# Fifteen rectified copies for a piecewise-linear GELU, on ScalarE in place of GpSimd

## The chip, the core and the metric

The kernel runs on one core of a Trainium2 chip. A core has engines with queues of their own: PE (TensorE, matrix products), DVE (VectorE), ACT (ScalarE), POOL (GpSimd) and SP (SyncE, which here only issues transfers). Each works through its own instructions in order and waits for the others by semaphores. All data that they work on lie in on-chip memory, 128 partitions wide; the products of PE land in PSUM. The metric is the time of one execution on the device in microseconds (us), and of several executions the median.

## The reference

The program is a chain of twelve residual steps on an x of 128 tokens by 256 features, in four layers of three steps: cross attention against a context of 12544 rows, self attention, and a feed-forward. Everything is in float32. The step that is changed is the feed-forward of the third layer (called l2f, since layers count from 0):

```python
_PWL_X = jnp.linspace(-4.0, 4.0, 33, dtype=jnp.float32)
_PWL_Y = 0.5 * _PWL_X * (1.0 + jax.lax.erf(_PWL_X / jnp.sqrt(jnp.float32(2.0))))
...
y = jnp.interp(xq, _PWL_X, _PWL_Y)
y = jnp.where(xq > 4.0, xq, jnp.where(xq < -4.0, jnp.float32(0.0), y))
...
h = jnp.einsum('bsd,df->bsf', x, w1) + b1
h = float2fix(h, MANT_BITS)
h = pwlin_gelu_basic(h, MANT_BITS, MANT_BITS)
h = float2fix(h, MANT_BITS)
out = jnp.einsum('bsf,fd->bsd', h, w2) + b2
return float2fix(out, MANT_BITS)
```

`float2fix` rounds to multiples of 1/256. The hidden width is 1024, so h has 128 tokens by 1024 values. The GELU is a broken line with a kink every 0.25 from −4 to 4.

## The kernel before

`Net` keeps x in on-chip memory and runs the twelve steps one after the other. Each step begins with a layer norm of x (`norm`, L271: statistics on DVE, a square root on ACT, and at L279 the scaled result on DVE), and turns it over to have features on partitions (`transposed`, L282). Products go through `mm` (L303). At the end `add_to_x` (the addition at L341) makes the new x. So a step can't start its own computation before the step ahead of it has ended.

What can run ahead are the keys and values of the four cross attentions (l0x, l1x, l2x, l3x), which depend on the context alone. They are split into jobs (`project`, L184): PE products, an ACT pass with a bias for the keys (L202), and POOL's transfers to scratch in device memory (L206 for keys, L230 for values). Jobs are taken from a list by `pump` (L136): within the cross attentions at given rates, and in the steps between them one job per PSUM bank asked for (`one`, L121). `weight` (L249) loads the weights of a step through POOL's transfer queue, two entries of the plan ahead, into three buffers; a load waits until the last reader of its buffer is done.

A cross attention (`cross`) first computes the queries, then scores of four groups of heads against 25 blocks of 512 context rows: maxima (score products at L447, reduced by DVE at L460), then the scores again, transposed (L495), exponentials on ACT (L508) and products with the values (L542). Before that POOL clears tiles for the keys (`clear`, memset at L392, 128x1024 each, up to 17 of them), zeroes small ones (L376, L380), and SP loads the keys back (L408).

The feed-forward l2f works on tiles of 128x1024, hidden features on partitions and tokens along the row, eight chunks of 128. It writes the broken line as an even part and a linear part. With a = min(|h|, 4) and kinks at 0, 0.25, ..., 3.75, it starts from y = h/2 and adds c_i · max(a − at_i, 0) for each of the sixteen kinks. The kink at zero needs no rectified copy, since a is never negative. For the other fifteen, POOL makes the copy (L1082) in a tile of the pool `l2f_r`, which has two buffers, and DVE adds it into y (L1084). Each sum needs the sum before it, and each copy needs a buffer that a sum has left. A mask `far` (L1074, L1088) replaces the result by max(h, 0) beyond 4 (L1086, L1087, L1090, L1091). Then y is rounded (`fixed`, L1043 and L1045), and sixteen matrix products give the output l2f_o, after which l3x begins.

The order of instructions on each engine is the program's order, but a scheduler moves instructions of different streams between each other: on POOL eight key transfers of l3x stand between the copies, one behind each pair.

Of the kernel before, what the change touches and what calls it, by code (L numbers as in the profile page):

```python
# [10 lines left out]
F32 = mybir.dt.float32  # L11
I32 = mybir.dt.int32
AF = mybir.ActivationFunctionType
ALU = mybir.AluOpType
# [4 lines left out]
P = 128  # L19
# [49 lines left out]
def _gelu_kinks():  # L69

    at = [0.25 * i for i in range(17)]
    even = [0.5 * a * math.erf(a / math.sqrt(2.0)) for a in at]
    slope = [(even[i + 1] - even[i]) / 0.25 for i in range(16)]
    return [(at[i], slope[i] - (slope[i - 1] if i else 0.0)) for i in range(16)]


class Net:
    def __init__(self, ctx, tc, io):
        self.tc, self.nc, self.io = tc, tc.nc, io
        nc = self.nc  # L80
        cp = ctx.enter_context(tc.tile_pool(name="const", bufs=1))
        self.small = ctx.enter_context(tc.tile_pool(name="small", bufs=2))
        self.xp = ctx.enter_context(tc.tile_pool(name="x", bufs=2))
        self.wp = ctx.enter_context(tc.tile_pool(name="w", bufs=3))
        self.bp = ctx.enter_context(tc.tile_pool(name="bg", bufs=2))
        self.dp = ctx.enter_context(tc.tile_pool(name="scratch", bufs=1, space=DRAM))
        self.ps1 = ctx.enter_context(tc.tile_pool(name="ps1", bufs=1, space=PSUM))
        self.psa = ctx.enter_context(tc.tile_pool(name="psa", bufs=1, space=PSUM))

        self.x = self.xp.tile([P, D], F32, name="x0", tag="x")  # L90
        nc.sync.dma_start(out=self.x, in_=io["x"])
        self.cst = cp.tile([P, NCONST], F32, name="cst", tag="cst")
        nc.sync.dma_start(out=self.cst, in_=io["cst"])
        self.cols = cp.tile([P, NCOL], F32, name="cols", tag="cols")
        nc.scalar.dma_start(out=self.cols, in_=io["cols"])
        self.rows = cp.tile([P, NROW], F32, name="rows", tag="rows")
        nc.gpsimd.dma_start(out=self.rows, in_=io["rows"].to_broadcast([P, NROW]))
        self.eps = {}
        for e in (EPS, 1e-6):
            t = cp.tile([P, 1], F32, name=f"eps{len(self.eps)}", tag=f"eps{len(self.eps)}")  # L100
            nc.vector.memset(t, e)
            self.eps[e] = t
        self.ident = self.const("ident")

        self.plan, self.tiles, self.loaded = [], {}, 0
        self.jobs, self.every, self.count, self.side = [], 0, 0, False
        self.turn, self.done = 0, set()
# [940 lines left out]
    def l2_ffn(self):  # L1048

        nc = self.nc  # L1050
        with self.tc.tile_pool(name="l2f", bufs=1) as pool, \
                self.tc.tile_pool(name="l2f_r", bufs=2) as rp:
            xn, xnT = self.normed(pool, "l2f")
            w1 = self.weight(("w_l2f1", None)).rearrange("p (c f) -> p c f", c=2)
            w2 = self.weight(("w_l2f2", None)).rearrange("p (c f) -> p c f", c=8)
            h = pool.tile([P, 8, P], F32, name="l2f_hs", tag="h")
            for i in range(2):
                ps = self.one(f"l2f_h{i}")
                for f in range(4):
                    ws = slice((4 * i + f) * P, (4 * i + f + 1) * P)  # L1060
                    self.mm(ps[:, f * P : (f + 1) * P], [w1[:, c, ws] for c in range(2)],
                            [xnT[:, c, :] for c in range(2)])
                b1 = self.col("l2f_b1")[:, 4 * i : 4 * i + 4]
                nc.vector.tensor_tensor(
                    out=h[:, 4 * i : 4 * i + 4, :], in0=ps.rearrange("p (c t) -> p c t", c=4),
                    in1=b1.unsqueeze(2).to_broadcast([P, 4, P]), op=ALU.add)
            h = h.rearrange("p c t -> p (c t)")
            self.fixed(h, h)

            a = pool.tile([P, 1024], F32, name="l2f_a", tag="a")  # L1070
            nc.vector.scalar_tensor_tensor(out=a, in0=h, scalar=-1.0, in1=h, op0=ALU.mult,
                                           op1=ALU.max)
            far = pool.tile([P, 1024], F32, name="l2f_far", tag="far")
            nc.vector.tensor_scalar(out=far, in0=a, scalar1=4.0, scalar2=None, op0=ALU.is_gt)  # L1074
            nc.vector.tensor_scalar(out=a, in0=a, scalar1=4.0, scalar2=None, op0=ALU.min)
            y = pool.tile([P, 1024], F32, name="l2f_y", tag="y")
            nc.vector.tensor_scalar(out=y, in0=h, scalar1=0.5, scalar2=None, op0=ALU.mult)
            for i, (at, c) in enumerate(_gelu_kinks()):
                t = a
                if i:  # L1080
                    t = rp.tile([P, 1024], F32, name=f"l2f_k{i}", tag="k")
                    nc.gpsimd.tensor_scalar(out=t, in0=a, scalar1=-at, scalar2=0.0, op0=ALU.add,  # L1082
                                            op1=ALU.max)
                nc.vector.scalar_tensor_tensor(out=y, in0=t, scalar=c, in1=y, op0=ALU.mult,  # L1084
                                               op1=ALU.add)
            nc.vector.tensor_scalar(out=h, in0=h, scalar1=0.0, scalar2=None, op0=ALU.max)  # L1086
            nc.vector.tensor_tensor(out=h, in0=h, in1=far, op=ALU.mult)  # L1087
            nc.vector.tensor_scalar(out=far, in0=far, scalar1=-1.0, scalar2=1.0, op0=ALU.mult,  # L1088
                                    op1=ALU.add)
            nc.vector.tensor_tensor(out=y, in0=y, in1=far, op=ALU.mult)  # L1090
            nc.vector.tensor_tensor(out=y, in0=y, in1=h, op=ALU.add)  # L1091
            self.fixed(y, y)
            ps = self.one("l2f_o")
            self.mm(ps[:, :D], [y[:, f * P : (f + 1) * P] for f in range(8)],
                    [w2[:, f, :] for f in range(8)])
            o = pool.tile([P, D], F32, name="l2f_os", tag="o")
            nc.vector.tensor_tensor(out=o, in0=ps[:, :D], in1=self.row("l2f_b2"), op=ALU.add)
            self.fixed(o, o)
            self.add_to_x([o], "l2f")
# [321 lines left out]
```

## Time and profile before

| | |
|---|---|
| median of 3 timed runs | 2828.08 us (2827.34 to 2830.71) |
| profiled execution, its own time | 2820.92 us |
| its span, first to last instruction | 2819.2 us |
| mean clock granted to TensorE | 0.931 of full |
| busy: PE, DVE, ACT, POOL | 2574.5, 1586.2, 1128.1, 695.3 us |
| between 2165 and 2256 us: PE, DVE, ACT, POOL busy | 14.33, 39.65, 3.52, 69.03 us |
| the same stretch: granted clock, share of the transfer engines | 0.57, 0.15 |

The first rows are for the whole program. The last two are for the stretch that holds l2f, 91 us long. In the profile a line such as L1084 is the line of the kernel before. A group of instructions is written as output<-inputs with shapes; "busy, mean ns" is their own time, and "idle before" is how long their engine stood still ahead of them and what released it. The chain that ended last is followed back from the last instruction of the program, at each step to what released it; "issue" in it is time for which the profile names no releaser.

### The profile page before, as it was taken

To read this page: it belongs to the slowest core of one execution; us is meant where nothing else is said; L and a number is where in the kernel's file an instruction comes from. 1 tells how busy PE (TensorE), PEld (TensorE's weight loads), DVE (VectorE), ACT (ScalarE), POOL (GpSimd) and SP (SyncE) were. 2 spreads that over 40 slices of the span, in tenths; PEclk is the share of its full clock that TensorE was granted. 3 is DMA by queue.
4 is the path that set the end of the run, shared out by engine and by line. 5 is a ranking of instruction groups with operands and counts; after the bars stand their busy time and mean duration, and the time that the engine had idled before them with its cause. 6 is when DMAs were issued, how large, how long until landed. Compare 5 with 4: busy or idle time off the path is not lost. (4 is left out here: it accounts for less than half of the span.)

```text
span 2819.2 us, 76052 instructions
## 1 busy us (share of the span) xinstructions
PE 2574.5 (91%) x32135; PEld 1882.8 (67%) x32135; DVE 1586.2 (56%) x3135; ACT 1128.1 (40%) x2076; POOL 695.3 (25%) x1287
## 2 busy tenths in 40 slices
PE   7999999998999999999998987999997089999978
PEld 4556887876745666666666555788886056888857
DVE  2445666413165788888776329666633376666422
ACT  1112555562202444444761340355564002555653
POOL 5775000014425222212123332000002824000001
PEclk9998999999978999999999995899999569999989
DMA  7875232226756766677544553222323034222216
GB/s 258 244 212 161 72 105 80 64 85 214 231 178 196 227 194 210 195 208 199 166 141 129 175 177 87 87 83 72 85 63 116 23 90 130 73 81 79 59 37 211
DMA packets 186355, 387.47 MB, mean 137 GB/s; under 512 B 32460, under 2 KB 88992, under 8 KB 181920
## 3 DMA queue, kind: packets, MB, share of 16 engines
q1 hardware_dynamic: 134064, 219.94, 25.9%
q0 software_dynamic: 51584, 161.42, 19.2%
q8 instruction: 255, 4.18, 0.6%
q10 hardware_dynamic: 368, 1.25, 0.1%
q14 instruction: 84, 0.69, 0.1%
HBM read 276.31 MB, written 112.58 MB: 138 GB/s over the span
## 5 line engine op out<-in xcount | busy, mean ns | idle before, releaser
L508 ACT ACTIVATE l1x_e<-l1x_e 128x512 f32<-128x512 f32 (+1 forms) x400 | 239.4, 621 | 254.7 <-DVE l1x_e L503 253.7
L460 DVE TENSOR_REDUCE l0x_mxs<-l0x_s 128x1 f32<-128x512 f32 (+1 forms) x400 | 243.7, 672 | 150.9 <-PE l0x_s L447 150.0
L455 DVE CUSTOM_DVE_ANT_0 l1x_j<-l1x_s,l1x_f 128x512 f32<-128x512 f32 (+1 forms) x400 | 271.5, 679 | 72.9 <-PE l1x_s L447 27.1
L460 DVE TENSOR_REDUCE l3x_mxs<-l3x_s 128x1 f32<-128x512 f32 (+1 forms) x400 | 242.4, 671 | 104.7 <-PE l3x_s L447 103.8
L508 ACT ACTIVATE l2x_e<-l2x_t 128x512 f32<-128x512 f32 (+1 forms) x400 | 206.4, 597 | 226.9 <-PE l2x_t L495 225.2
L460 DVE TENSOR_REDUCE l2x_mxs<-l2x_s 128x1 f32<-128x512 f32 (+1 forms) x400 | 241.9, 671 | 95.1 <-PE l2x_s L447 94.2
L503 DVE TENSOR_TENSOR l1x_e<-l1x_t,l1x_g 128x512 f32<-128x512 f32 (+1 forms) x400 | 249.6, 673 | 62.5 <-ACT l1x_e L508 31.2
L508 ACT ACTIVATE l0x_e<-l0x_t 128x512 f32<-128x512 f32 (+1 forms) x400 | 206.3, 597 | 163.6 <-PE l0x_t L495 161.9
L508 ACT ACTIVATE l3x_e<-l3x_t 128x512 f32<-128x512 f32 (+1 forms) x400 | 206.2, 597 | 156.8 <-PE l3x_t L495 155.1
L495 PEld LDWEIGHTS l1x_t<-l1x_qb,l1x_kt 32*128 32x128 f32 x3136 | 171.1, 187 | 81.3 <-ACT l2x_vs L225 27.6
L495 PE MATMUL l0x_t<-l0x_qb,l0x_kt 32*128 32x128 f32 x3136 | 206.1, 283 | 5.8 <-ACT l0x_e L508 5.8
L495 PE MATMUL l2x_t<-l2x_qb,l2x_kt 32*128 32x128 f32 x3136 | 205.9, 283 | 5.7 <-ACT l2x_e L508 5.6
L495 PE MATMUL l3x_t<-l3x_qb,l3x_kt 32*128 32x128 f32 x3136 | 204.7, 283 | 5.8 <-ACT l3x_e L508 5.8
L495 PE MATMUL l1x_t<-l1x_qb,l1x_kt 32*128 32x128 f32 x3136 | 204.7, 285 | 4.2 <-ACT l2x_vs L225 1.2
L495 PEld LDWEIGHTS l0x_t<-l0x_qb,l0x_kt 32*128 32x128 f32 x3136 | 178.0, 187 | 39.6 <-issue 21.8
L495 PEld LDWEIGHTS l2x_t<-l2x_qb,l2x_kt 32*128 32x128 f32 x3136 | 177.9, 187 | 38.9 <-issue 21.4
L495 PEld LDWEIGHTS l3x_t<-l3x_qb,l3x_kt 32*128 32x128 f32 x3136 | 176.8, 186 | 38.4 <-issue 20.4
L447 PE MATMUL l2x_s<-l2x_kt,l2x_qb 32*128 32x512 f32 (+1 forms) x800 | 200.3, 741 | 0.5 <-issue 0.5
L447 PE MATMUL l3x_s<-l3x_kt,l3x_qb 32*128 32x512 f32 (+1 forms) x800 | 194.7, 695 | 2.3 <-ACT l3x_ks L202 1.8
L206 POOL DMA_DIRECT2D l3x_kx<-l3x_ks x208 | 100.1, 489 | 332.0 <-ACT l3x_ks L202 294.1
L447 PE MATMUL l0x_s<-l0x_kt,l0x_qb 32*128 32x512 f32 (+1 forms) x800 | 176.7, 654 | 4.5 <-ACT l0x_ks L202 4.5
L447 PE MATMUL l1x_s<-l1x_kt,l1x_qb 32*128 32x512 f32 (+1 forms) x800 | 173.3, 657 | 3.2 <-DMA l1x_kt<-l1x_kx 1.9
(609 smaller groups left out, 4058.2 us busy)
## 6 DMA issues: line engine op xcount, KB each, us to landing
l1x_f<-in_fside SPq DMA_DIRECT2D x96, 256.0 KB
l1x_g<-in_fsideT SPq DMA_DIRECT2D x96, 256.0 KB
w<-in_w_l3f POOLq DMA_DIRECT2D x16, 1024.0 KB, 5.1
l0x_kt<-l0x_kx SPq DMA_DIRECT2D x192, 72.0 KB
l1x_kt<-l1x_kx SPq DMA_DIRECT2D x192, 72.0 KB
l2x_kt<-l2x_kx SPq DMA_DIRECT2D x192, 72.0 KB
l3x_kt<-l3x_kx SPq DMA_DIRECT2D x192, 72.0 KB
l0x_vx<-l0x_vs POOLq DMA_DIRECT2D x24, 544.0 KB, 7.2
```

The costliest lines, as they stand in the source:

```text
L206: nc.gpsimd.dma_start(out=kx[8 * half + h, 2:18, :], in_=t["k"][16 * h : 16 * h + 16, :n])
L447: nc.tensor.matmul(banks[j][:, :m], qb[g][r, :], t[r, at : at + m], start=True, stop=True)
L455: nc.vector.tensor_tensor_reduce(out=junk[:, :m], in0=banks[j][:, :m], in1=ft[k][:, :m], scale=1.0, scalar=-3.0e38, op0=ALU.add, op1=ALU.m ...
L460: nc.vector.tensor_reduce(out=mxs[g][:, j, i : i + 1], in_=banks[j][:, :m], axis=AX.X, op=ALU.max)
L495: nc.tensor.matmul(banks[j][:, a * P : (a + 1) * P], t[r, at + a * P : at + (a + 1) * P], qb[g][r, :], start=True, stop=True)
L503: nc.vector.tensor_tensor(out=e[:, j, :m], in0=src, in1=gt[k][:, : m // P, :].rearrange("p a q -> p (a q)"), op=ALU.add)
L508: nc.scalar.activation(e[:, j, :m], src, AF.Exp)
```

## The change

There are three edits. A constant tile `kinks` of 128x16 is filled at the start by POOL, one column per kink with the value −at_i, which stands on POOL's queue ahead of the first weight loads. The pool of the rectified copies gets three buffers in place of two, 4 KB per partition more. The copies are made by ACT as Relu(a + bias), with a column of `kinks` as the bias, where POOL computed max(a − at_i, 0). The sums on DVE and everything on PE stay as they are, in the same order; on ACT the fifteen copies come between the last key pass ahead of l2f_o and the square root of l3x's norm.

```diff
         self.ident = self.const("ident")
+        self.kinks = cp.tile([P, 16], F32, name="kinks", tag="kinks")
+        for i, (at, _) in enumerate(_gelu_kinks()):
+            nc.gpsimd.memset(self.kinks[:, i : i + 1], -at)
...
         with self.tc.tile_pool(name="l2f", bufs=1) as pool, \
-                self.tc.tile_pool(name="l2f_r", bufs=2) as rp:
+                self.tc.tile_pool(name="l2f_r", bufs=3) as rp:
...
                 t = a
                 if i:
                     t = rp.tile([P, 1024], F32, name=f"l2f_k{i}", tag="k")
-                    nc.gpsimd.tensor_scalar(out=t, in0=a, scalar1=-at, scalar2=0.0, op0=ALU.add,
-                                            op1=ALU.max)
+                    nc.scalar.activation(t, a, AF.Relu, bias=self.kinks[:, i : i + 1])
                 nc.vector.scalar_tensor_tensor(out=y, in0=t, scalar=c, in1=y, op0=ALU.mult,
                                                op1=ALU.add)
```

## The prediction

> **What bounds the kernel now.** I read the page first, from the top: busy times, then the 40 slices of 70.5 us.
>
> ```profile
> PE 2574.5 (91%) x32135; PEld 1882.8 (67%) x32135; DVE 1586.2 (56%) x3135; ACT 1128.1 (40%) x2076; POOL 695.3 (25%) x1287
> ...
> PE   7999999998999999999998987999997089999978
> ...
> ACT  1112555562202444444761340355564002555653
> POOL 5775000014425222212123332000002824000001
> PEclk9998999999978999999999995899999569999989
> ```
>
> Over the whole span PE decides. One slice contradicts this: the 32nd (2185 to 2255 us) has PE at 0, ACT at 0 and POOL at 8. It is the second layer's feed-forward (l2f), where the change is made. So I left the averages and asked for the groups of instructions between 2175 and 2256 us (busy and mean | idle before, and who ended it), and for VectorE's timeline there.
>
> ```profile
> L1082 POOL TENSOR_SCALAR l2f_k<-l2f_a 128x1024 f32<-128x1024 f32 x15 | 60.2, 4023 | 8.2 <-DVE l2f_a L1075 7.8
> L1084 DVE SCALAR_TENSOR_TENSOR l2f_y<-l2f_k,l2f_y 128x1024 f32<-128x1024 f32 x15 | 23.4, 1557 | 38.3 <-POOL l2f_k L1082 38.3
> ```
>
> ```profile
> 2180.39 2.05 DVE L1084 SCALAR_TENSOR_TENSOR l2f_y<-l2f_a,l2f_y 128x1024 f32<-128x1024 f32 x1
> 2182.37 0.68 DVE L1088 TENSOR_SCALAR l2f_far<-l2f_far 128x1024 f32<-128x1024 f32 x1
> 2183.99 2.05 DVE L1084 SCALAR_TENSOR_TENSOR l2f_y<-l2f_k,l2f_y 128x1024 f32<-128x1024 f32 x1 [0.94 <-POOL l2f_k L1082]
> 2187.58 1.22 DVE L1084 SCALAR_TENSOR_TENSOR l2f_y<-l2f_k,l2f_y 128x1024 f32<-128x1024 f32 x1 [1.54 <-POOL l2f_k L1082]
> ...
> 2243.49 1.23 DVE L1084 SCALAR_TENSOR_TENSOR l2f_y<-l2f_k,l2f_y 128x1024 f32<-128x1024 f32 x1 [3.52 <-POOL l2f_k L1082]
> 2244.75 1.23 DVE L1090 TENSOR_TENSOR l2f_y<-l2f_y,l2f_far 128x1024 f32<-128x1024 f32 x1
> 2246.01 1.23 DVE L1091 TENSOR_TENSOR l2f_y<-l2f_y,l2f_hs 128x1024 f32<-128x1024 f32 x1
> ```
>
> Each sum into y waits for POOL's kink, all 15 times, 38.3 us in all. Some sums take 2.05 us instead of 1.22: those during which POOL was also working. Two dependent operations of this size with POOL quiet start 1.26 us apart (2244.75, 2246.01).
>
> Does the time after l2f follow from l2f's end? The chain that ended last says so (start, duration, what):
>
> ```profile
> 2173.49 75.31 issue
> 2248.79 6.38 PE l2f_o L306 x16
> ...
> 2257.97 9.45 DVE l3x_xn L279
> ...
> 2268.79 3.76 PE l3x_q L306 x16
> ...
> 2273.03 33.59 PE l3x_s L447 x111
> ```
>
> PE has nothing for 75 us; no projection is left that was queued ahead. After it come x, the norm, the queries and the scores, one behind the other, until PE is full again. A microsecond off l2f is then a microsecond off the end, unless something else is late at 2258.
>
> **What the Trainium skill says.** "ScalarE: Activation LUTs", What ACT_TABLE_LOAD costs: an ACTIVATE with a bias read from a [128,1] operand takes about 280 + 0.833·N ns whatever the function, and successive ones overlap by about 93 ns. The trace agrees: L202 with such a bias has means of 474 ns at 256 and 686 ns at 512 elements, 0.83 ns an element. The same page, Table sets, says relu is in every table set; here the compiled ACT stream has no table load at the kinks, nor at l3x's Sqrt behind them. "SBUF — State Buffer", Terms: VectorE and GpSimd lock a shared port pair for a whole instruction, ACT has its own ports. The 2.05 us sums and the 9.45 us L279, whose own length elsewhere is 0.41, agree. "TensorE: Matmul & The Clock Gate", Part 1: after about 3.4 us idle the clock halves and needs about as long busy to return. Here it fell by 2176, 2.5 us after the last matmul.
>
> **The change part by part.**
>
> 1. VectorE's loop. Without POOL the first sum, at 2180.39, takes 1.23 instead of 2.05, so L1088 starts at 2181.55 and the first kink's sum at about 2182.15 (such neighbours start 0.60 apart). Fifteen sums at 1.26 are 18.9 us, so L1090 starts at 2201.05 instead of 2244.75: 43.7 us gone. Cross-check by busy and idle: 23.4 + 38.3 − 18.9 = 42.8, and 0.8 from the first sum, 43.6. I take 43.6.
>
> 2. ScalarE's kinks. By the skill's price an estimate of 280 + 0.833·1024 = 1133 ns each; by L202's slope 686 + 424 = 1110. `l2f_a` is ready at 2179.33, so the first kink is ready at 2180.5, before VectorE wants it. Both prices are below 1.26, so VectorE sets the pace. With three buffers kink i+3 may start when sum i ends and is wanted 2.5 us later; it needs 1.2. ACT is idle for 87.9 us there, so nothing queues behind it but l3x's Sqrt, which needs VectorE's result anyhow. Bounds: at 1.0 a kink nothing changes; at 1.5, ACT leads and 15 × 0.24 = 3.6 us come back.
>
> 3. POOL. Gone are 15 instructions of 4.0 us. Eight writes of l3x's keys, which stood between them (0.5 us each, up to 2243.4), now go out in one row from 2171.7, and the weight load for l3a behind them leaves at about 2177 instead of 2243.93. Neither was waited for: the key block is read by the SP loads at 2318, l3a comes after l3x. The next weight load (l3f) waits for l2f_o's matmuls, and POOL's memsets for l3x wait for x. Both move with l2f's end.
>
> 4. What is late next. The start of l3x keeps its faults: l2f_o on a half clock (PE still idle for 32 us), then L279, locked out while POOL clears ten l3x_kt tiles. In the new program the first of these memsets has eight more waits on DMA rings. If that delayed it past L279's start, 9 us would go. But l2x's start already has this wait, seven rings and PE, and there the order is the same:
>
> ```profile
> 1693.15 0.19 POOL L376 MEMSET l2x_zero<- 1x128 f32 x1 [10.78 <-issue]
> ...
> 1693.58 15.23 POOL L392 MEMSET l2x_kt<- 128x1024 f32 x17
> ...
> 1694.33 14.63 DVE L279 TENSOR_SCALAR l2x_xn<-l1f_x,l2x_mv,l2x_r 128x256 f32<-128x256 f32 x1
> ```
>
> The memset comes 0.43 us after l2x_zero there, and 0.43 in l3x (2256.85, 2257.28). The waits cost nothing, so L279 stays locked out: 0.
>
> 5. The sixteen memsets of the constant stand on POOL before the first weight load (1.94 us). Four of the same shape start 0.035 us apart: 0.6 us in all; if each waited for its 0.10, 1.6. The first queries wait for that load (to 14.42), but PE then stands 0.99 us until 19.16 for the context. That slack hides 0.6 and leaves 0.6 of 1.6. I take 0.
>
> Sum: 2820.9 us, the profiled execution's own time (span 2819.2), − 43.6 = 2777.3. The median of the timed runs lies 7.2 us above that execution, and a saving is the same in both: 2828.1 − 43.6 = **2784.5**.
>
> **Rivals.**
>
> - *The sums do not get shorter, or ACT leads.* If VectorE's sums stay at 2.05 because ACT reads the same tile, 15 × 0.83 + 0.8 = 13 us come back: 2797.5. An ACT pace of 1.5 gives 2788. For it: no trace row has the two together on such tiles. Against: 1.22 occurs whenever POOL rests.
> - *L279 escapes the memsets.* 9 us more: 2775.5. For it: 0.7 us decide. Against: l2x.
> - *PE's clock returns at another moment.* In 2285 to 2312 the clock was half again although PE had work; the values' matmuls at 2306 took 3.7 us for 8 against 1.7 later, and scores 2.0 against 1.1. So 3 us may go or be added: 2781 to 2788. l2f_o and the queries keep about the cold 6.4 and 3.8.
> - *The other side: the first kink waits.* It now waits, at ACT's head, for all eight rings of SP's queue, the kinks memset and `l2f_a`. A ring whose awaited transfer lands late holds every kink and l3x's Sqrt. From 43.6 us on, a landing after about 2223, it eats the gain; at 60 the time is 2844. Against: POOL's first kink waited for the same eight rings and began at 2179.51, 0.18 us after `l2f_a`. No SP transfer is issued between 2162 and 2258.
>
> **How the numbers follow.** Main case with the clock's play, 2779 to 2790: 0.73. Sums or ACT slower, 2790 to 2800: 0.13. L279 free, 2771 to 2779: 0.10. The kink's wait: 0.02 slower, 0.01 just balanced. Unseen gain: 0.01. The three timed runs spread over 3.4 us. The range 2774 to 2794 keeps the main case and the nearer parts of its neighbours, about 0.85. A difference of 0.2%, 5.7 us, is about what this measurement can tell from none. Faster 0.97, same 0.01, slower 0.02.
>
> **What would show it.** ACT rows of l2f_k at about 1.1 us, fifteen, no table load; VectorE's sums all 1.22, 1.26 apart, with no idle on ACT beyond the first; PE's hole 32 us instead of 75; L279 still about 9.4; equal gaps from l2f_o to the first scores. Wrong if ACT's first kink starts well after L1075, if sums show 2.05, if the first l3x scores wait for a key tile, or if the stages after 2700 gain or lose by themselves.

## The result and the profile after

The changed kernel takes 2781.57 us, the median of four runs (2778.88 to 2784.97), against 2827.71 us for the kernel before on the same chip (four runs, 2826.30 to 2830.71). The ratio is 0.9836, with a 95% interval of 0.9819 to 0.9853: 42 to 51 us less. The profiled execution took 2778.88 us by its own time, with a span of 2777.1 us, 42.1 less than that of before.

First the page of the kernel after: the busy times, and the rows of the 40 slices, which are 69.4 us long now.

```profile
PE 2573.6 (93%) x32135; PEld 1881.1 (68%) x32135; DVE 1580.7 (57%) x3135; ACT 1145.7 (41%) x2091; POOL 639.0 (23%) x1288
...
PE   7998999998989999999997995999999499999968
...
ACT  1112555572212344444572231155557302555643
POOL 5775000004535122221214343000000323000000
PEclk9998999999978999999999996699999768999989
```

The busy time moved as ordered: ACT has 15 instructions and 17.6 us more, POOL 56.3 us less. In the 32nd slice (2152 to 2222 us) PE is at 4 instead of 0, because the hole around l2f now fits inside it with work on either side.

The groups of the kernel after between 2170 and 2215 us (busy and mean | idle before, and who ended it):

```profile
L1086 DVE SCALAR_TENSOR_TENSOR l2f_y<-l2f_k,l2f_y 128x1024 f32<-128x1024 f32 x15 | 18.4, 1224 | 1.5
L1085 ACT ACTIVATE l2f_k<-l2f_a,kinks 128x1024 f32<-128x1024 f32 x15 | 17.0, 1147 | 12.6 <-DVE l2f_a L1078 9.9 <-DVE l2f_y L1086 2.6
```

Lines stand three lower here than before up to the copy itself (L1085 makes the copies, L1086 sums). No sum waits for a copy any more: of the 38.3 us of idle before the sums 1.5 are left, and no releaser is named for these. It is ACT that waits for the sums, 2.6 us in all. And no sum takes 2.05 us: the mean is 1224 ns where it was 1557.

The timeline of the same stretch, start and duration in us:

```profile
2181.12 3.23 ACT L1085 ACTIVATE l2f_k<-l2f_a,kinks 128x1024 f32<-128x1024 f32 x3 [9.95 <-DVE l2f_a L1078]
2182.02 1.21 DVE L1086 SCALAR_TENSOR_TENSOR l2f_y<-l2f_a,l2f_y 128x1024 f32<-128x1024 f32 x1
2183.15 0.68 DVE L1090 TENSOR_SCALAR l2f_far<-l2f_far 128x1024 f32<-128x1024 f32 x1
2183.75 19.82 DVE L1086 SCALAR_TENSOR_TENSOR l2f_y<-l2f_k,l2f_y 128x1024 f32<-128x1024 f32 x15
2185.00 1.15 ACT L1085 ACTIVATE l2f_k<-l2f_a,kinks 128x1024 f32<-128x1024 f32 x1 [0.65 <-DVE l2f_y L1086]
...
2203.61 1.22 DVE L1092 TENSOR_TENSOR l2f_y<-l2f_y,l2f_far 128x1024 f32<-128x1024 f32 x1
...
2207.65 6.07 PE L309 MATMUL l2f_o<-w,l2f_y 128*128 128x256 f32 x16 [32.54 <-issue]
...
2215.85 8.98 POOL L395 MEMSET l3x_kt<- 128x1024 f32 x10
...
2216.53 9.45 DVE L282 TENSOR_SCALAR l3x_xn<-l2f_x,l3x_mv,l3x_r 128x256 f32<-128x256 f32 x1
...
2224.78 0.20 POOL L219 MEMSET l3x_vs<- 128x64 f32 x1
2224.87 0.96 POOL L395 MEMSET l3x_kt<- 128x1024 f32 x1
...
2227.30 3.78 PE L309 MATMUL l3x_q<-l3x_xnT,w 128*128 128x128 f32 x16 [0.52 <-DVE l3x_xnT L296]
...
2231.58 33.59 PE L450 MATMUL l3x_s<-l3x_kt,l3x_qb 32*128 32x512 f32 x112 [0.49 <-issue]
```

Where the time went can be read off two marks. From the end of `l2f_a` (2180.95; 2179.33 before) to the start of the product with `far` (2203.61; 2244.75 before) it is 22.7 us, and it was 65.4: 42.8 us gone, in this one place. From the start of l2f_o to the first score of l3x it is 23.93 us, and it was 24.24: nothing else moved. The fifteen sums fill 19.82 us, so they start (19.82 − 1.22) / 14 = 1.33 us apart; that is more than the 1.26 of two dependent neighbours before, with no wait on ACT to show for it. This, the missing need of a third buffer, and what is left in the stretch are what the runs below look at.

### The profile page after: what moved, and what is told of

Its sections match the earlier page's. It is cut to its first block, busy times and chain, and to the rows that moved or that the text cites. A ratio compares the mean times of both kernels' runs of the same rounds, so it can differ in the third digit from the quotient of the medians.

```text
span 2777.1 us, 76067 instructions
## 1 busy us (share of the span) xinstructions
PE 2573.6 (93%) x32135; PEld 1881.1 (68%) x32135; DVE 1580.7 (57%) x3135; ACT 1145.7 (41%) x2091; POOL 639.0 (23%) x1288
```

## The experiments

Each has the edit against the kernel before or after. A time beside it is the median of the timed runs, with the ratio to the kernel before on the same chip.

### The third buffer without ACT

The kernel before, with POOL making the copies, and three buffers instead of two.

```diff
-                self.tc.tile_pool(name="l2f_r", bufs=2) as rp:
+                self.tc.tile_pool(name="l2f_r", bufs=3) as rp:
```

> The kernel before with the third buffer alone; the copies stay on POOL. Theory (POOL's 4.0 us a copy and its hold on VectorE's port set the pace): POOL was busy 60.2 us of the 64 between the first and the last copy, so a buffer more changes nothing: 2825 to 2830 us, copies still about 4.0 us each. Rival (the two buffers made POOL and VectorE take turns, and the third frees them): clearly faster, 2800 or less.

Measured: 2821.89 us against 2825.86, ratio 0.9985 (0.9979 to 0.9992). So the buffer is worth 2 to 6 us on POOL, a small part of the change's 46, and not nothing. The groups of this kernel in l2f:

```profile
L1082 POOL TENSOR_SCALAR l2f_k<-l2f_a 128x1024 f32<-128x1024 f32 x15 | 58.2, 3894 | 7.5 <-DVE l2f_a L1075 7.2
L1084 DVE SCALAR_TENSOR_TENSOR l2f_y<-l2f_k,l2f_y 128x1024 f32<-128x1024 f32 x15 | 27.2, 1814 | 30.4 <-POOL l2f_k L1082 30.4
```

From the first copy to the product with `far` it is now 61.2 us (2184.17 to 2245.34) where it was 65.2. Two things make these 4 us. Three key transfers stand between the copies instead of seven (the eighth came behind the last copy), since the scheduler puts one behind every four or five copies here and behind every two before: 4 × 0.55 = 2.2 us of POOL. And the copies take 3894 ns instead of 4023: 15 × 0.13 = 1.9 us. Of the 7.9 us that VectorE saves in waiting (38.3 to 30.4) it gives back half, since more sums now take 2.05 us (mean 1814 ns instead of 1557). POOL's speed is the bound with three buffers as with two.

### ACT with two buffers

The kernel after, with two buffers.

```diff
-                self.tc.tile_pool(name="l2f_r", bufs=3) as rp:
+                self.tc.tile_pool(name="l2f_r", bufs=2) as rp:
```

> The changed kernel with two buffers in place of three. Theory: a copy starts when the sum before last ends, and takes 1.15 us and 0.18 us of hand-over, just as long as the sum that runs meanwhile (1.33 us); so the pace is 1.33 to 1.4 us and the time 0 to 1.5 us above the changed kernel's 2781.6. Rival (with two buffers copy and sum take turns, 1.15 + 1.22 + hand-overs, about 2.6 us a kink): 15 to 19 us slower than the changed kernel, about 2799.

Measured: 2780.59 us, ratio 0.9840 (0.9825 to 0.9854), no different from the change itself. The sums fill 19.83 us, 1.33 apart, and ACT waits for them 3.9 us instead of 2.6. The third buffer brings nothing once ACT makes the copies, and the whole gain belongs to the change of engine.

### The copies on VectorE itself

Is it ACT's help that pays, or POOL's absence? Here VectorE makes the copies, with the instruction that POOL had.

```diff
-                    nc.scalar.activation(t, a, AF.Relu, bias=self.kinks[:, i : i + 1])
+                    nc.vector.tensor_scalar(out=t, in0=a, scalar1=-at, scalar2=0.0, op0=ALU.add,
+                                            op1=ALU.max)
```

> The changed kernel with the copies made by VectorE itself, so that no engine helps it. Theory (what cost was POOL, not the want of a helper): a copy is a one-input operation of 0.69 us, as the other ones of this size, so a kink costs 0.7 + 1.2 to 1.3 = 1.9 to 2.0 us in place of 1.33: 15 x 0.6 = 8 to 10 us slower than the changed kernel, 2790 to 2792, and still some 36 us faster than before. Rival (the gain comes from having the copies on another engine beside VectorE's sums): most of the gain is lost, 2815 or more.

Measured: 2787.84 us, ratio 0.9862 (0.9845 to 0.9878), which is 6.3 us above the change and 38.0 us below the kernel before on the same chip (2825.86). The intervals of this ratio and of the change's just overlap, so the 6.3 us rest on the trace: from `l2f_a` to the product with `far` it is 29.0 us (2183.50 to 2212.46), 6.3 more than with ACT and 36.5 less than before. The groups:

```profile
L1087 DVE SCALAR_TENSOR_TENSOR l2f_y<-l2f_k,l2f_y 128x1024 f32<-128x1024 f32 x15 | 18.3, 1221 | 0.0
L1085 DVE TENSOR_SCALAR l2f_k<-l2f_a 128x1024 f32<-128x1024 f32 x15 | 10.2, 688 | 0.0
```

The same instruction takes 688 ns on VectorE and 3894 to 4023 on POOL. So VectorE alone does copy and sum in 1.74 us a kink, where with POOL's help it took (2243.49 − 2183.99) / 14 = 4.25. Six sevenths of the gain in this stretch (36.5 of 42.8 us) come from taking POOL out, and ACT adds the rest. The loss is smaller than expected because a copy now stands between two sums: each sum then starts 1.13 us ahead of the next instruction, not 1.26 or 1.33, and the copy that the scheduler puts there takes only 0.60 more.

### ACT with fifteen buffers

Why are the sums 1.33 us apart? If the cause is the handing back of buffers, it goes away when every copy has its own.

```diff
-                self.tc.tile_pool(name="l2f_r", bufs=3) as rp:
+                self.tc.tile_pool(name="l2f_r", bufs=15) as rp:
```

> The changed kernel with fifteen buffers, so that ScalarE never waits for VectorE. In the changed kernel the sums start 1.33 us apart, where the prediction had 1.26. Theory (each sum waits for two semaphores, VectorE's own and ScalarE's, and the second costs about 0.07 us even when long fulfilled): still 1.33 us apart. Rival (ScalarE's copy, kept back by the third buffer, is what comes last): 1.26 us apart, 1 us less in all.

Measured: 2784.76 us in its one timed run. Its timeline:

```profile
2182.95 15.70 ACT L1085 ACTIVATE l2f_k<-l2f_a,kinks 128x1024 f32<-128x1024 f32 x15 [9.95 <-DVE l2f_a L1078]
...
2185.58 19.82 DVE L1086 SCALAR_TENSOR_TENSOR l2f_y<-l2f_k,l2f_y 128x1024 f32<-128x1024 f32 x15
```

ACT runs through without a pause, a copy every (15.70 − 1.14) / 14 = 1.04 us, and is done at 2198.65. The sums take 19.82 us as before, and the last five of them, whose copies had long been there, keep the same pace. Buffers and ACT are not the cause.

### Two running sums

If it is the need of each sum for the one just ahead, then two sums in turn, added at the end, take it away. The first odd kink starts `y2` with a product alone.

```diff
+            y2 = pool.tile([P, 1024], F32, name="l2f_y2", tag="y2")
...
-                nc.vector.scalar_tensor_tensor(out=y, in0=t, scalar=c, in1=y, op0=ALU.mult,
+                if i == 1:
+                    nc.vector.tensor_scalar(out=y2, in0=t, scalar1=c, scalar2=None, op0=ALU.mult)
+                    continue
+                s = y2 if i % 2 else y
+                nc.vector.scalar_tensor_tensor(out=s, in0=t, scalar=c, in1=s, op0=ALU.mult,
                                                op1=ALU.add)
+            nc.vector.tensor_tensor(out=y, in0=y, in1=y2, op=ALU.add)
```

> The changed kernel with two running sums in turn, one for the even and one for the odd kinks, added at the end. Theory (of the 1.33 us between two sums, 1.13 is the operation, 0.13 is that it needs the result just ahead of it, and 0.07 the second wait): sums start 1.13 to 1.2 us apart. With one sum turned into a product of 0.69 us and one addition of 1.26 more, the loop from the first kink's sum to the end of the addition is about 1 to 2 us shorter, too little to see in the time. Rival (1.33 us is what the operation takes beside a busy ScalarE): still 1.33 apart, and the loop some 0.7 us longer.

Measured: 2779.78 us in its one timed run. The timeline:

```profile
2183.25 0.68 DVE L1088 TENSOR_SCALAR l2f_y<-l2f_k 128x1024 f32<-128x1024 f32 x1
2183.86 15.97 DVE L1091 SCALAR_TENSOR_TENSOR l2f_y<-l2f_k,l2f_y 128x1024 f32<-128x1024 f32 x14
2199.75 0.68 DVE L1096 TENSOR_SCALAR l2f_far<-l2f_far 128x1024 f32<-128x1024 f32 x1
2200.35 1.22 DVE L1093 TENSOR_TENSOR l2f_y<-l2f_y,l2f_y 128x1024 f32<-128x1024 f32 x1
2201.60 1.23 DVE L1098 TENSOR_TENSOR l2f_y<-l2f_y,l2f_far 128x1024 f32<-128x1024 f32 x1
```

Fourteen sums in 15.97 us start (15.97 − 1.22) / 13 = 1.13 us apart, though each still takes a copy from ACT. From the sum of the zero kink on, with the change of `far` in it in both, the loop takes 18.35 us (2183.25 to 2201.60) where the change has 20.46 (2183.15 to 2203.61): 2.1 us less, in spite of one addition more. So the whole gap from 1.13 to 1.33 goes with the need for the result just ahead. The one time can't show 2 us; the trace does.

### POOL's clears behind the norm of l3x

What remains in the stretch is L282: 9.45 us for a norm that takes 0.41 elsewhere, while POOL clears key tiles. In the timeline above it ends at 2225.98, 0.15 us after an eleventh clear of a key tile (2224.87 to 2225.83), not after the row of ten. Here POOL writes its zero row as 0 · xn, so that it can't begin on l3x before the norm is there; the tiles and their contents stay the same.

```diff
-            nc.gpsimd.memset(zero, 0.0)
+            if name in ("l3x",):
+                nc.gpsimd.tensor_scalar(out=zero, in0=xn[0:1, :P], scalar1=0.0, scalar2=None,
+                                        op0=ALU.mult)
+            else:
+                nc.gpsimd.memset(zero, 0.0)
```

> The changed kernel, where in l3x POOL's first small clear reads the normalised x, so that POOL's ten clears of key tiles come after the norm's last operation on VectorE and not beside it. Theory (that operation takes 9.45 us because POOL holds the shared port, and all that follows waits for it): 0.4 us for it, and first scores 8 to 9 us earlier; 2772 to 2774 us. Rival (the first scores then wait for the cleared and loaded key tile, which are now later): the operation is short, but first scores and end move by less than 3 us.

Measured: 2776.50 us, ratio 0.9820 (0.9805 to 0.9835), 5.1 us below the change. The two intervals overlap, so the times alone don't show these 5 us. The timeline:

```profile
2217.48 0.41 DVE L282 TENSOR_SCALAR l3x_xn<-l2f_x,l3x_mv,l3x_r 128x256 f32<-128x256 f32 x1
...
2218.86 8.98 POOL L399 MEMSET l3x_kt<- 128x1024 f32 x10
2218.97 3.10 PE L309 MATMUL l3x_q<-l3x_xnT,w 128*128 128x128 f32 x16 [0.52 <-DVE l3x_xnT L296]
...
2222.55 18.38 PE L454 MATMUL l3x_s<-l3x_kt,l3x_qb 32*128 32x512 f32 x62 [0.49 <-POOL l3x_kt L399]
```

The norm takes 0.41 us, and from the new x to the first score it is 6.7 us (2215.82 to 2222.55) where it was 16.7: 10.0 us, more than expected. From x to the end of l3x, 8.3 us of them are left (453.5 us for 461.8). Then 2 us go at l3f, where a row of twenty products takes 4.30 us instead of 2.50: PE's clock was still at half there. So the mechanism is right, and the size in the total is short of the 8 to 9 expected. That the norm waits because POOL's clears run beside it is shown by their order alone; what the two engines share there, no run looked at.

### The same in l2x

The same edit with l2x in the list; its norm took 14.64 us, beside seventeen clears.

```diff
-            if name in ("l3x",):
+            if name in ("l2x", "l3x"):
```

> The same in l2x as well, where the norm's operation takes 14.6 us beside seventeen clears. Theory: another 13 to 14 us, 2758 to 2761 us. Rival (scores there catch up with key tiles whose clears and loads come later): l2x gives less than 5 us.

Measured: 2760.86 us (2756.81 to 2764.77), ratio 0.9760 (0.9744 to 0.9777), 20.7 us below the change and 15.6 below the version with l3x alone. The timeline:

```profile
1702.71 0.41 DVE L282 TENSOR_SCALAR l2x_xn<-l1f_x,l2x_mv,l2x_r 128x256 f32<-128x256 f32 x1
...
1704.07 15.23 POOL L399 MEMSET l2x_kt<- 128x1024 f32 x17
...
1708.72 27.35 PE L454 MATMUL l2x_s<-l2x_kt,l2x_qb 32*128 32x512 f32 x92 [0.49 <-POOL l2x_kt L399]
```

From x to the first score it is 7.7 us (21.9 in the change), and from x to the end of l2x 438.6 us instead of 451.9: 13.3 us, as expected, and in the same place as the edit.

### The sums on PE

PE stands still in l2f, so it could add: the identity scaled by c_i times the i-th copy, seventeen products per half tile into one bank. ACT makes ten copies, VectorE five, in fifteen buffers. This stands on the version with both clears behind the norm.

```diff
+            for i, c in enumerate([0.5] + [c for _, c in kinks]):
+                nc.scalar.activation(scaled[:, i, :], self.ident, AF.Copy, scale=c)
...
+            def add(i, t):
+                for j in range(2):
+                    nc.tensor.matmul(ps[j], scaled[:, i, :], t[:, j * 512 : (j + 1) * 512],
+                                     start=(i == 0), stop=(i == 16))
...
-                nc.vector.scalar_tensor_tensor(out=y, in0=t, scalar=c, in1=y, op0=ALU.mult,
-                                               op1=ALU.add)
+                add(i + 1, t)
```

> The kernel with both norms freed, and the sixteen kinks added up by PE: products of scaled identity matrices with the copies, accumulated in two PSUM banks; ten copies by ScalarE, five by VectorE. Theory (VectorE's chain of sums sets l2f's length, and PE's idle time there is what halves its clock): the 34 products of 128x512 take 0.43 us each on a full clock, 14.6 us, against 19.9 us of sums, and begin sooner, so l2f_o starts 6 to 9 us earlier; it then takes 3.4 us instead of 6.1, and the queries may take 1.8 instead of 3.8. In all 8 to 13 us below the kernel with both norms freed, about 2747 to 2752. Rival (the products run at half clock, 0.86 us each, 29 us): 5 to 9 us slower than that kernel.

Measured: 2771.20 us (2762.99 to 2771.66), ratio 0.9795 (0.9779 to 0.9811), some 10 us above the version that it stands on, where the theory expected a gain. The timeline:

```profile
2175.97 25.91 PE L1092 MATMUL l2f_y<-l2f_k,l2f_c 128*128 128x512 f32 x60
...
2205.39 6.75 PE L309 MATMUL l2f_o<-w,l2f_y 128*128 128x256 f32 x16 [3.50 <-DVE l2f_y L1052]
```

and the busy time by stretch (us and instructions of each engine, then the granted clock, the transfers' share and GB/s):

```profile
2165.00:2200.00 35.00, 32.91 (x99) 16.01 (x98) 10.77 (x15) 12.01 (x14) 6.32 (x11) 1.00 0.23 61
2200.00:2205.00 5.00, 1.89 (x5) 0.57 (x3) 3.66 (x5) 0.00 (x0) 0.00 (x0) 0.97 0.00 0
2205.00:2210.00 5.00, 4.61 (x11) 3.68 (x12) 0.33 (x1) 0.00 (x0) 0.00 (x0) 0.50 0.00 0
```

The thirty products of 128x512 are sixty records of 0.43 us, so one product is 0.86 us and not the 0.43 that the theory had taken for it, and this on the full clock. (The eight products of l2f_o in the source likewise stand as sixteen records.) A kink costs PE 1.73 us, more than VectorE's 1.33; from the turned norm of l2f to its new x it is 49.2 us instead of 44.2, which is half of the loss; the rest was not traced to a place. Nor did a busy PE keep the clock for l2f_o: after 3.5 us without a product it was at 0.50 again, and l2f_o took 6.75 us.

### Clears behind the norm and two running sums

The two gains that held, together: the edits of the two running sums and of the clears in l2x and l3x.

> The changed kernel with POOL's clears of l2x and l3x behind the norm and with two running sums in l2f. If the two gains lie one behind the other on the same chain, as theory has it, the sums take 1.5 us off the version with the clears alone (2760.9): about 2759, and in the trace the 14 sums start 1.13 us apart and both norms last 0.41 us. The rival: PE's clock, which comes back at other moments, moves more than that, so the time may lie anywhere from 2755 to 2765 although both parts show in the trace.

Measured: 2756.37 us (2755.55 to 2761.40, five runs) against 2825.09, ratio 0.9758 (0.9742 to 0.9775). Both parts are in the trace: fourteen sums in 15.97 us, and norms of 0.41 us in l2x and l3x. In l2f the loop takes 18.35 us, 2.1 less than with one sum, and l2f_o 5.52 instead of 6.15. The interval overlaps that of the version with the clears alone, so the timed runs don't tell the two apart; 2.1 us is what the trace shows. It is the fastest kernel here, and against the changed one the clears are what matters.

## Why the prediction was right

The forecast was 2784.5 us, the time is 2781.57. The gap between the two profiled executions is 42.0 us (2820.92 to 2778.88), where 43.6 were forecast. By the steps of the prediction:

1. *VectorE's loop.* The first sum took 1.21 us as forecast, no sum took 2.05, and the stretch from `l2f_a` to the product with `far` lost 42.8 us for 43.6. The mis-sized term is the pace: 15 × 1.26 was 15 × 1.33 in fact, 1.0 us more. The 1.26 was read from two instructions that depend on each other and wait for no other engine. The sums do both, and the chain of the kernel after shows what stands between two of them (start, duration, what; DVEq is VectorE's queue):

```profile
2183.75 1.22 DVE l2f_y L1086
2184.98 0.03 issue
2185.00 0.02 DVEq L1086
2185.03 0.04 issue
2185.07 1.24 DVE l2f_y L1086
```

   Fifteen buffers did not remove the gap, and two running sums did. That it is the dependence is shown. The 0.07 us beyond 1.26 lie where a wait of its own, 0.02 us on the queue, stands between two sums: the next sum starts 0.10 us after the record ahead of it, while the product with `far` starts 0.03 us after the last sum (2203.57 to 2203.61). That the second wait is their cause is still argued: no run took that wait alone away, and the pairs at 1.26 end in another instruction than a sum.

   The prediction's reading of the 2.05 us is loose. It gives them to the sums during which POOL was working, but almost all sums ran beside a copy, and what decided was which of the two started first. Two places of the kernel before:

```profile
2192.27 3.62 POOL L1082 TENSOR_SCALAR l2f_k<-l2f_a 128x1024 f32<-128x1024 f32 x1
2192.32 2.06 DVE L1084 SCALAR_TENSOR_TENSOR l2f_y<-l2f_k,l2f_y 128x1024 f32<-128x1024 f32 x1 [3.52 <-POOL l2f_k L1082]
...
2200.66 1.22 DVE L1084 SCALAR_TENSOR_TENSOR l2f_y<-l2f_k,l2f_y 128x1024 f32<-128x1024 f32 x1 [3.52 <-POOL l2f_k L1082]
2200.70 4.66 POOL L1082 TENSOR_SCALAR l2f_k<-l2f_a 128x1024 f32<-128x1024 f32 x1
```

   A sum behind the start of a copy grew by 0.83 us; a sum ahead of it kept its 1.22, and the copy grew instead. So the 2.05 us do not agree with a lock on a shared port for a whole instruction, as the prediction has it: behind a copy of 3.6 us that would have cost a sum more than 3 us. The forecast did not suffer, since without POOL every sum takes 1.22 either way.

2. *ScalarE's kinks.* 1147 ns in the mean, 1.04 us apart where nothing holds them; forecast 1110 to 1133. No table load stands among them. VectorE sets the pace, as forecast, and two buffers do as well as three.

3. *POOL.* The key transfers left in one row from 2173.94, nine of them, and the load for l3a behind them at 2179.24; nothing waited for either. The run with three buffers on POOL corrects one thing in the picture of before: the transfers between the copies, and so the order that the scheduler chose, were themselves worth about 2 us there.

4. *What is late next.* Held to 0.3 us: PE's hole was 32.54 us, l2f_o took 6.07 (6.36 before), L282 9.45, the queries 3.78, and the first score came 23.93 us after l2f_o's start. The eight new waits of the first clear cost nothing, as in l2x: it came 0.43 us after `l3x_zero`, as before. The clears that held L282 were eleven, not the ten that the prediction counts.

5. *The sixteen memsets at the start.* They took 0.62 us and put the first weight load from 1.94 to 2.45; the first queries came at 14.47 instead of 14.42, and the context's keys at 19.18 instead of 19.16. Nothing, as taken.

The sum of the profiled executions closes with two terms that no step had: l2f began 1.6 us later (2171.26 for 2169.65), since x of l1f was already 3.2 us late in a part of the program that the change doesn't touch, and from l2f's new x to the end it took 0.7 us less. With the loop and the 0.3 of l2f_o that is 1.6 − 42.8 − 0.3 − 0.7 = −42.2, against −42.1 in the spans. That the two new terms partly cancel is luck. The profiled execution came out 1.6 us above its forecast (2778.88 for 2777.3) and the median 2.9 below. The reason is that the forecast took the same distance between the two for before and after: it was 7.2 us before and is 2.7 after. The saving by medians is 46.1, by profiles 42.0; both lie in the interval of 42 to 51, and these runs can't decide between them.

Of the rivals, the slower sums or a leading ACT, the freed L279 and the late ring did not come; the clock of PE may have moved, but l2f_o (0.3 us less) and all that follows l2f's new x (0.7 us less) leave it less than the 3 us allowed. The two runs that order the clears behind the norm show what the freed L279 would have brought: 8.3 us by the end of l3x, near the 9 worked out, and 5 in the total.

## What to carry to other kernels

Before an elementwise step is given to POOL as a helper, price it by its own row in a trace: here one instruction took 4.0 us there and 0.69 on VectorE, so that VectorE alone was 38 us faster than with that help. When one stage shows an idle PE while the span shows it nearly full, read that stage by itself, fix what its waits name, and then look for what stands behind it: POOL's clears ahead of a norm were worth another 20 us and no line of the diff touched them. Where a pace of dependent instructions goes into a sum, take it from instructions that have the same waits.

## What the runs showed of the hardware

- *The pace of VectorE's instructions depends on what the next one needs.* For 128x1024 in float32 with two inputs the record is 1.22 us throughout, but the starts are 1.13 us apart when the next one doesn't need the result, 1.26 when it does, and 1.33 for the sums, which also take their other operand from ACT. The Trainium skill, "Perfetto Trace Analysis", Optimizing Scalar/DVE Operations, says that half of an instruction's fixed overhead, the acknowledgement of the write, overlaps the next instruction. The 0.09 us by which the independent sums overlap agree with it in kind; for that half the page gives about 60 ns. A dependent one starts 0.03 us after the record ahead of it has ended, and a sum that also waits for ACT 0.10 us after.
- *POOL and VectorE make each other longer, and the one that starts second pays.* In the kernel before, six of the fifteen sums started 0.05 us behind a copy: these took 2.05 us and the copies 3.61. Eight started ahead of one: these took 1.22 us and the copies 4.19 to 4.66. With three buffers this holds for all sums but one (2.62 us).
- *One short instruction waits for a whole row of POOL's.* L282 did not slip in between two clears, in l3x for eleven (9.45 us) or in l2x for seventeen (14.64 us). It was done in 0.41 us when POOL began after it, and the rows of ten and seventeen clears took their 8.98 and 15.23 us all the same.
- *PE's clock comes back at other moments for the same work.* l2f_o took between 5.45 and 6.15 us in the kernels with a pause of 30 to 33 us ahead of it, and the queries of l3x behind it 3.10 to 3.79. The Trainium skill, "TensorE: Matmul & The Clock Gate", Part 1, says that the window over which activity is judged runs freely and is not started by the kernel. These spreads agree with that: a gain of some us may be followed by a loss of two elsewhere, as at l3f.
- *A product in float32 of 128x512 is two records of 0.43 us*, 0.86 us on the full clock; the price of one record is half that of the product.
